# A four-way column and row scan: the order of batches, rows and columns of the map in SBUF

## The chip, the cores and the metric

The kernel runs on one core of a Trainium2 chip. A core has five engines that run at the same time and wait for each other by semaphores: TensorE (matrix products, PE in the profile, with its weight loads as PEld), VectorE (DVE), ScalarE (ACT), GpSimd (POOL) and SyncE (SP, which here issues the DMAs). Tiles lie in SBUF, whose 128 partitions each hold a row of bytes; products land in PSUM. The metric is the device time of one execution in microseconds; less is better. All data is fp32.

## The reference

The input x has the shape [32 batches, 48 channels, 64 rows, 128 columns]. Two layers follow each other, each x = x + scan(groupnorm(x)). The scan of a layer goes over the map four times: down the rows, up the rows, right over the columns, left over the columns. Each step adds to a row (or column) a 5-tap convolution, over the other axis and all channels, of the row (or column) before it:

```python
def step(w, b):
    def f(carry, inp):
        nxt = inp + _conv1d(carry, w, b)   # 48 -> 48 channels, 5 taps, padding 2
        return (nxt, nxt)
    return f
...
xs = jnp.moveaxis(x, 2, 0)
d0 = xs[0]
_, d_rest = jax.lax.scan(step(down_w, down_b), d0, xs[1:])
D = jnp.concatenate([d0[None], d_rest], 0)
seq = jnp.concatenate([D[Hh - 3::-1], D[Hh - 1:Hh]], 0)
u0 = D[Hh - 1]
_, u_rest = jax.lax.scan(step(down_w, down_b), u0, seq)
...
ws = jnp.moveaxis(jnp.moveaxis(U, 0, 2), 3, 0)
_, r_rest = jax.lax.scan(step(right_w, right_b), r0, ws[1:])
...
_, l_rest = jax.lax.scan(step(left_w, left_b), l0, R[Ww - 2::-1])
...
x = x + _L0_conv_ref(_gn(x), ...)
x = x + _L1_conv_ref(_gn(x), ...)
```

The steps of a scan depend on each other, and so do the four scans and the two layers. The 32 batches are independent.

## The kernel before

**Layout.** Positions along the convolved axis go in pairs. The channels of the even position lie on partitions 0 to 47, those of the odd position on 64 to 111, zeros between (`SIDES`). One convolution step is then three accumulated 112 x 112 products (L173, L174, L177): with the pair itself, the pair before and the pair after. Each product appears twice in the trace, as two passes of TensorE over the same columns.

**Chains and lanes.** Four batches (G = 4) make a chain, whose steps are done together: a step in the down and up scans has 4 x 64 = 256 columns (64 pairs of columns of the map), one in the right and left scans 4 x 32 = 128 (32 pairs of rows). Eight chains go in two lanes: lane 0 has chains 0, 2, 4, 6 and lane 1 has 1, 3, 5, 7. The lanes are written step by step in turn, so that lane 1's products run while lane 0's step is finished on VectorE, and the other way round. Tile names carry chain, layer and scan: `ps_7L0d` is chain 7, layer 0, down.

**The map.** Each lane has one map (L75) that holds a chain's four batches, and the scans run in place on it. Its free dimensions are [batch G, pair of columns WP = 64, parity r, pair of rows HP = 32], 64 KB a partition. `row(h)`, L194, is a step's operand in down and up: 256 values, each 256 bytes from the next within a batch. `col(v)`, L197, is that of right and left: four runs of 32 values. `last` (L79) and the carries of the up scan are packed tiles of their own, [G, WP].

**A step** (`step`, L168) is the three products into a PSUM tile and one VectorE operation (L180) that adds bias and input and writes the result. In down it reads and writes the map; the last step writes `last`. In up the products read the packed carry, VectorE reads a row of the map and writes the next carry, and ScalarE copies each carry to where the other layout has it (`place`, L184, two copies a step, L188). In right and left VectorE reads and writes columns of the map.

**Between the scans.** Per batch: the input x is loaded to a tile [112, 32 pairs of rows, 128 columns] (L98, SyncE's queue), `add_scan` (L105) adds the map to it on GpSimd, `store_x` writes it out (L103), `stats` (L110) forms scale and offset of the group norm on VectorE, TensorE and ScalarE, and `normalize` (L148) writes the normalized batch into the map: four instructions, two on ScalarE (L152) for the even columns and two on GpSimd (L159) for the odd ones. From layer 0 to 1 the normalized batch is the one that was just added; from layer 1 the next chain's batch is loaded instead. The order of each engine's queue is laid down when the program is built, and each engine takes its instructions in that order.

Of the kernel before, what the change touches and what calls it, by code (L numbers as in the profile page):

```python
"""Two pre-activation layers x + scan(groupnorm(x)), each scan running down, up, right and
left over the feature map with a 5-tap convolution across the other axis per step.

Layout. Channels of even and odd positions along the convolved axis sit side by side on the
partitions (even at 0..47, odd at 64..111, zeros between), so that one convolution step is
three accumulated 112 x 112 matrix products: with the pair before, the pair itself and the
pair after. The map of a batch lies in SBUF as [pair of w][r][pair of h]:
  down/up:     partition side = parity of w, r = parity of h
  right/left:  partition side = parity of h, r = parity of w
The scans run in place; the up scan writes its rows to where the second layout has them.  # L10

Batches go in chains of G, and two chains are in flight step by step in turn, so that what
a step of one chain waits for runs under the other's matrix products.
"""
# [1 line left out]

# [5 lines left out]
F32 = mybir.dt.float32  # L22
AF = mybir.ActivationFunctionType
ALU = mybir.AluOpType
# [3 lines left out]
P = ODD + C  # L28
# [3 lines left out]
G = 4  # L32
# [7 lines left out]
def kernel(  # L40
# [31 lines left out]
        for i in range(LANES)  # L72
    ]
    maps = [
        cpool.tile([P, G, WP, 2, HP], F32, tag=f"map{i}", name=f"map{i}")  # L75
        for i in range(LANES)
    ]
    lasts = [
        cpool.tile([P, G, WP], F32, tag=f"last{i}", name=f"last{i}") for i in range(LANES)  # L79
    ]  # L80
    mid = dram.tile([B, C, H, W], F32, tag="mid", name="mid")

    # The partitions between the two sides carry zeros throughout.
    for i, t in enumerate(maps + [xt for lane in xts for xt in lane]):
        eng = nc.vector if i % 2 else nc.gpsimd
        eng.memset(t[32:64], 0.0)
# [5 lines left out]
        return ap[b].rearrange("c (q r) w -> r c q w", r=2)[side]  # L92

    def load_x(lane: int, src: bass.AP, b: int) -> bass.AP:
        """Batch j of a chain always goes to tile j % NX of its lane."""
        xt = xts[lane][b % G % NX]
        for side in range(2):
            nc.sync.dma_start(xt[SIDES[side]], rows(src, b, side))  # L98
        return xt
# [3 lines left out]
            nc.sync.dma_start(rows(dst, b, side), xt[SIDES[side]])  # L103

    def add_scan(lane: int, j: int, xt: bass.AP):  # L105
        nc.gpsimd.tensor_tensor(  # L106
            xt, xt, maps[lane][:, j].rearrange("c p r q -> c q (p r)"), ALU.add
        )

    def stats(xt: bass.AP, key: str):  # L110
        """Per-partition scale and offset of the group norm of one batch."""

        def small(n, name):
            return stat_pool.tile([P, n], F32, tag=name, name=f"{name}_{key}")

        st = stat_pool.tile([P, NSEG, 6], F32, tag="st", name=f"st_{key}")
        flat = xt.rearrange("c q w -> c (q w)")
        for s in range(NSEG):
            nc.vector.bn_stats(st[:, s, :], flat[:, bass.ts(s, SEG)])  # L119
        mv = small(2, "mv")  # L120
        nc.vector.bn_aggr(mv, st.rearrange("c s k -> c (s k)"))  # L121
        ps = ps_stat.tile([P, 2], F32, tag="ps_stat", name=f"ps_stat_{key}")
        nc.tensor.matmul(ps[:, 0:1], mask_sb, mv[:, 0:1], start=True, stop=True)  # L123
        mean = small(1, "mean")
        nc.vector.tensor_copy(mean, ps[:, 0:1])
        dev = small(1, "dev")
        nc.vector.tensor_sub(dev, mv[:, 0:1], mean)
        sq = small(1, "sq")
        nc.vector.scalar_tensor_tensor(sq, dev, dev, mv[:, 1:2], ALU.mult, ALU.add)  # L129
        nc.tensor.matmul(ps[:, 1:2], mask_sb, sq, start=True, stop=True)  # L130
        var = small(1, "var")
        nc.vector.tensor_scalar(var, ps[:, 1:2], GN_EPS, None, ALU.add)  # L132
        # 1 / sqrt(var), with a Newton step behind the table's square root.
        std = small(1, "std")
        nc.scalar.activation(std, var, AF.Sqrt)  # L135
        r0 = small(1, "r0")
        nc.vector.reciprocal(r0, std)
        t0 = small(1, "t0")
        nc.vector.scalar_tensor_tensor(t0, var, r0, r0, ALU.mult, ALU.mult)
        t1 = small(1, "t1")  # L140
        nc.vector.tensor_scalar(t1, t0, -0.5, 1.5, ALU.mult, ALU.add)
        scale = small(1, "scale")
        nc.vector.tensor_mul(scale, r0, t1)
        offset = small(1, "offset")
        nc.vector.scalar_tensor_tensor(offset, mean, -1.0, scale, ALU.mult, ALU.mult)  # L145
        return scale, offset

    def normalize(lane: int, j: int, xt: bass.AP, scale: bass.AP, offset: bass.AP):  # L148
        view = xt.rearrange("c q (p r) -> c p r q", r=2)
        for hs in range(2):  # L150
            hsl = SIDES[hs]
            nc.scalar.activation(  # L152
                maps[lane][SIDES[0], j, :, hs, :],
                view[hsl, :, 0, :],
                AF.Identity,
                bias=offset[hsl],
                scale=scale[hsl],
            )
            nc.gpsimd.tensor_scalar(  # L159
                maps[lane][SIDES[1], j, :, hs, :],  # L160
                view[hsl, :, 1, :],
                scale[hsl],
                offset[hsl],
                ALU.mult,
                ALU.add,
            )

    def step(lane: int, layer: int, way: int, key: str, prev, inp, dst):  # L168
        """dst = inp + conv(prev) + bias over [P, G, pairs]."""
        n = prev.shape[2]  # L170
        ps = ps_scan.tile([P, G, n], F32, tag=f"ps{lane}", name=f"ps_{key}")
        wt = w_sb[:, layer, way]
        nc.tensor.matmul(ps, wt[:, 1], prev, start=True, stop=False)  # L173
        nc.tensor.matmul(  # L174
            ps[:, :, 1:n], wt[:, 0], prev[:, :, 0 : n - 1], start=False, stop=False
        )
        nc.tensor.matmul(  # L177
            ps[:, :, 0 : n - 1], wt[:, 2], prev[:, :, 1:n], start=False, stop=True
        )
        nc.vector.scalar_tensor_tensor(  # L180
            dst, ps, b_sb[:, layer, way : way + 1], inp, ALU.add, ALU.add
        )

    def place(lane: int, h: int, carry: bass.AP):  # L184
        """Row h of the up scan to where the right and left scans read it."""
        q, hs = divmod(h, 2)
        for ws in range(2):
            nc.scalar.copy(maps[lane][SIDES[hs], :, :, ws, q], carry[SIDES[ws]])  # L188

    def scan(lane: int, layer: int, key: str, early):  # L190
        """The four scans of a layer. early() is called shortly before the end."""
        m, last = maps[lane], lasts[lane]

        def row(h):  # L194
            return m[:, :, :, h % 2, h // 2]

        def col(v):  # L197
            return m[:, :, v // 2, v % 2, :]

        for h in range(1, H):  # L200
            dst = row(h) if h < H - 1 else last
            step(lane, layer, DOWN, f"{key}d{h}", row(h - 1), row(h), dst)
            yield
        place(lane, H - 1, last)
        prev = last
        for h in range(H - 2, -1, -1):
            carry = carry_pool.tile(
                [P, G, WP], F32, tag=f"carry{lane}", name=f"carry_{key}u{h}"
            )
            inp = row(h - 1) if h else last  # L210
            step(lane, layer, DOWN, f"{key}u{h}", prev, inp, carry)
            place(lane, h, carry)
            prev = carry
            yield
        for v in range(1, W):
            step(lane, layer, RIGHT, f"{key}r{v}", col(v - 1), col(v), col(v))
            yield
        for v in range(W - 2, -1, -1):
            if v == 24:
                early()  # L220
            step(lane, layer, LEFT, f"{key}l{v}", col(v + 1), col(v), col(v))
            yield
# [43 lines left out]


def _weights(np, inputs):
    """[in side and channel, layer, way, pair offset, out side and channel]: the taps by
    the distance of the positions; zeros where the kernel does not reach."""  # L270
    w = np.zeros((P, 2, 3, 3, P), np.float32)
    b = np.zeros((P, 2, 3), np.float32)
    for layer in range(2):
# [11 lines left out]


def _group_mask(np):
    """Averages the partitions of a channel group, over both sides."""
    group = np.full(P, -1)
    for s in SIDES:  # L290
        group[s] = np.arange(C) // (C // GROUPS)
    same = (group[:, None] == group[None, :]) & (group[:, None] >= 0)
    return np.where(same, np.float32(GROUPS / (2 * C)), np.float32(0))
# [21 lines left out]
```

## Time and profile before

| | us |
|---|---|
| three runs, median (lowest, highest) | 8434.96 (8434.68, 8440.88) |
| profiled execution, span from the first to the last instruction | 8440.7 |
| chain 7, layer 0: down, first to first product load of the next scan | 315.4 |
| the same for up | 169.4 |
| the same for right | 172.6 |
| left, to its last product load | 168.8 |
| from there to chain 7's first product load in layer 1 | 200.1 |

The profiled execution's span is 5.7 us above the median of the runs and 0.2 below the highest of them; no other time is shown for it. TensorE is busy 6745.4 us (80% of the span), its weight loads 5026.5 (60%), VectorE 3721.4 (44%), ScalarE 1902.0 (23%), GpSimd 1264.6 (15%). The stages of the table come eight times, once for each pair of chains and each layer, with the two lanes interleaved. Shares over the whole span mix these stages; a row of the table of windows gives the busy times within one stage.

A group's row in the trace reads: line, engine, operation, output<-inputs, shapes, count | busy us, mean ns of one | idle time of the engine ahead of them and what ended it. A timeline row reads: start, length, engine, line, operation, and in brackets the idle time ahead with what ended it.

### The profile page before, as it was taken

To read this page: it belongs to the slowest core of one execution; us is meant where nothing else is said; L and a number is where in the kernel's file an instruction comes from. 1 tells how busy PE (TensorE), PEld (TensorE's weight loads), DVE (VectorE), ACT (ScalarE), POOL (GpSimd) and SP (SyncE) were. 2 spreads that over 40 slices of the span, in tenths; PEclk is the share of its full clock that TensorE was granted. 3 is DMA by queue.
4 is the path that set the end of the run, shared out by engine and by line. 5 is a ranking of instruction groups with operands and counts; after the bars stand their busy time and mean duration, and the time that the engine had idled before them with its cause. 6 is when DMAs were issued, how large, how long until landed. Compare 5 with 4: busy or idle time off the path is not lost. (4 is left out here: it accounts for less than half of the span.)

```text
span 8440.7 us, 85243 instructions
## 1 busy us (share of the span) xinstructions
PE 6745.4 (80%) x36736; PEld 5026.5 (60%) x36736; DVE 3721.4 (44%) x7235; ACT 1902.0 (23%) x2241; POOL 1264.6 (15%) x199
## 2 busy tenths in 40 slices
PE   4999559994499955999449995599944999559993
PEld 2479524894247952489424795248942479524893
DVE  5345533553334553355333455335532345533552
ACT  3070110700207011070020701107012070110700
POOL 4000330003300033000330003300043000330004
PEclk9999779997699977999769997799976999779997
DMA  9000240005700024000570002400057000340005
GB/s 94 0 1 1 44 76 0 1 1 74 105 0 1 1 41 79 0 1 1 75 105 0 1 1 46 74 0 1 1 75 105 0 1 1 46 74 0 1 1 90
DMA packets 497403, 258.09 MB, mean 31 GB/s; under 512 B 5392, under 2 KB 496912, under 8 KB 497024
## 3 DMA queue, kind: packets, MB, share of 16 engines
q1 hardware_dynamic: 496640, 251.68, 20.7%
q8 instruction: 287, 4.70, 0.2%
q10 hardware_dynamic: 384, 0.96, 0.0%
q14 instruction: 92, 0.75, 0.0%
HBM read 151.95 MB, written 100.66 MB: 30 GB/s over the span
## 5 line engine op out<-in xcount | busy, mean ns | idle before, releaser
L106 POOL TENSOR_TENSOR x<-x,map 112x4096 f32<-112x4096 f32 x64 | 694.3, 10866 | 6611.4 <-issue 3290.5
L123 PE MATMUL ps_stat_x<-mv_x,mask_sb 112*112 112x1 f32 x64 | 16.4, 326 | 728.1 <-DVE mv_x L121 722.2
L188 ACT COPY map<-last 48x256 f32<-48x256 f32 x32 | 21.9, 683 | 2469.5 <-DVE last L180 2469.2
L123 PEld LDWEIGHTS ps_stat_x<-mv_x,mask_sb 112*112 112x112 f32 x64 | 14.9, 286 | 731.8 <-DVE mv_x L121 724.8
L135 ACT ACTIVATE std_m<-var_m 112x1 f32<-112x1 f32 x32 | 6.5, 203 | 1850.4 <-DVE var_m L132 1850.3
L123 PE MATMUL ps_stat_m<-mv_m,mask_sb 112*112 112x1 f32 x64 | 16.4, 326 | 473.8 <-DVE mv_m L121 448.6
L119 DVE BATCH_NORM_STATS2 st_x<-x 112x6 f32<-112x512 f32 x256 | 155.6, 679 | 513.9 <-DMA x<-in_x 513.7
L135 ACT ACTIVATE std_x<-var_x 112x1 f32<-112x1 f32 x32 | 6.5, 203 | 1615.1 <-DVE var_x L132 1615.1
L159 POOL TENSOR_SCALAR map<-x,scale_x,offset_x 48x2048 f32<-48x2048 f32 x64 | 277.8, 4341 | 346.3 <-DVE offset_x L145 340.3
L119 DVE BATCH_NORM_STATS2 st_m<-x 112x6 f32<-112x512 f32 x256 | 160.5, 679 | 340.7 <-POOL x L106 340.7
L159 POOL TENSOR_SCALAR map<-x,scale_m,offset_m 48x2048 f32<-48x2048 f32 x64 | 271.6, 4244 | 195.4 <-DVE offset_m L145 171.3
L123 PEld LDWEIGHTS ps_stat_m<-mv_m,mask_sb 112*112 112x112 f32 x64 | 14.9, 286 | 477.7 <-DVE mv_m L121 450.7
L152 ACT ACTIVATE map<-x,offset_x,scale_x 48x2048 f32<-48x2048 f32 x64 | 279.3, 4364 | 44.9 <-DVE offset_x L145 41.3
L152 ACT ACTIVATE map<-x,offset_m,scale_m 48x2048 f32<-48x2048 f32 x64 | 273.1, 4268 | 51.6 <-DVE offset_m L145 34.1
L130 PE MATMUL ps_stat_m<-sq_m,mask_sb 112*112 112x1 f32 x64 | 16.5, 328 | 151.9 <-DVE sq_m L129 151.9
L180 DVE SCALAR_TENSOR_TENSOR map<-ps_1L1d,b_sb,map 112x256 f32<-112x256 f32 x62 | 75.3, 1215 | 123.7 <-PE ps_1L1d L177 117.9
L180 DVE SCALAR_TENSOR_TENSOR map<-ps_3L1d,b_sb,map 112x256 f32<-112x256 f32 x62 | 75.5, 1217 | 123.1 <-PE ps_3L1d L177 118.0
L180 DVE SCALAR_TENSOR_TENSOR map<-ps_7L0d,b_sb,map 112x256 f32<-112x256 f32 x62 | 76.3, 1231 | 121.2 <-PE ps_7L0d L177 115.6
L180 DVE SCALAR_TENSOR_TENSOR map<-ps_7L1d,b_sb,map 112x256 f32<-112x256 f32 x62 | 75.5, 1217 | 123.0 <-PE ps_7L1d L177 117.9
L180 DVE SCALAR_TENSOR_TENSOR map<-ps_5L1d,b_sb,map 112x256 f32<-112x256 f32 x62 | 75.4, 1216 | 123.0 <-PE ps_5L1d L177 117.9
L180 DVE SCALAR_TENSOR_TENSOR map<-ps_3L0d,b_sb,map 112x256 f32<-112x256 f32 x62 | 76.4, 1232 | 120.7 <-PE ps_3L0d L177 115.4
L180 DVE SCALAR_TENSOR_TENSOR map<-ps_5L0d,b_sb,map 112x256 f32<-112x256 f32 x62 | 76.3, 1231 | 120.6 <-PE ps_5L0d L177 115.5
(617 smaller groups left out, 19622.9 us busy)
## 6 DMA issues: line engine op xcount, KB each, us to landing
x<-in_x SPq DMA_DIRECT2D x128, 768.0 KB, 16.3
mid<-x SPq DMA_DIRECT2D x64, 768.0 KB, 12.1
x<-mid SPq DMA_DIRECT2D x64, 768.0 KB, 16.0
out<-x SPq DMA_DIRECT2D x64, 768.0 KB, 12.6
w_sb<-in_w ACTq DMA_DIRECT2D x1, 882.0 KB, 12.2
mask_sb<-in_mask ACTq DMA_DIRECT2D x1, 49.0 KB, 1.9
b_sb<-in_b ACTq DMA_DIRECT2D x1, 2.6 KB, 5.4
```

The lines of the kernel that those rows point to most:

```text
L106: nc.gpsimd.tensor_tensor(xt, xt, maps[lane][:, j].rearrange("c p r q -> c q (p r)"), ALU.add)
L119: nc.vector.bn_stats(st[:, s, :], flat[:, bass.ts(s, SEG)])
L123: nc.tensor.matmul(ps[:, 0:1], mask_sb, mv[:, 0:1], start=True, stop=True)
L130: nc.tensor.matmul(ps[:, 1:2], mask_sb, sq, start=True, stop=True)
L135: nc.scalar.activation(std, var, AF.Sqrt)
L152: nc.scalar.activation(maps[lane][SIDES[0], j, :, hs, :], view[hsl, :, 0, :], AF.Identity, bias=offset[hsl], scale=scale[hsl],)
L159: nc.gpsimd.tensor_scalar(maps[lane][SIDES[1], j, :, hs, :], view[hsl, :, 1, :], scale[hsl], offset[hsl], ALU.mult, ALU.add,)
L180: nc.vector.scalar_tensor_tensor(dst, ps, b_sb[:, layer, way : way + 1], inp, ALU.add, ALU.add)
L188: nc.scalar.copy(maps[lane][SIDES[hs], :, :, ws, q], carry[SIDES[ws]])
```

## The change

The map's free dimensions become [parity r, pair of columns, pair of rows, batch], so that the four batches of a chain lie side by side. `row(h)` is then 64 runs of four values (16 bytes), each run 512 bytes from the next; `col(v)` is one run of 128 values. `last`, the carries and the PSUM tiles follow: [pairs, batch]. The products with the pair before and after are shifted by one pair of four columns, so that their PSUM output is one run. `normalize` reads x along the columns in steps of 8 bytes and writes the map in steps of 512. `add_scan` becomes two instructions for each batch, one for each parity r, that read and write x in steps of 8 bytes and read the map in steps of 512. `place` writes rows of runs of 16 bytes. Sizes of tiles, loads, stores and the arithmetic stay. Comments are left out of the new file.

```diff
     maps = [
-        cpool.tile([P, G, WP, 2, HP], F32, tag=f"map{i}", name=f"map{i}")
+        cpool.tile([P, 2, WP, HP, G], F32, tag=f"map{i}", name=f"map{i}")
...
-        cpool.tile([P, G, WP], F32, tag=f"last{i}", name=f"last{i}") for i in range(LANES)
+        cpool.tile([P, WP, G], F32, tag=f"last{i}", name=f"last{i}") for i in range(LANES)
...
     def add_scan(lane: int, j: int, xt: bass.AP):
-        nc.gpsimd.tensor_tensor(
-            xt, xt, maps[lane][:, j].rearrange("c p r q -> c q (p r)"), ALU.add
-        )
+        for r in range(2):
+            half = xt.rearrange("c q (p r) -> c r q p", r=2)[:, r]
+            nc.gpsimd.tensor_tensor(half, half, maps[lane][:, r, :, :, j].rearrange("c p q -> c q p"), ALU.add)
...
     def normalize(lane: int, j: int, xt: bass.AP, scale: bass.AP, offset: bass.AP):
-        view = xt.rearrange("c q (p r) -> c p r q", r=2)
+        view = xt.rearrange("c q (p r) -> c r q p", r=2)
...
             nc.scalar.activation(
-                maps[lane][SIDES[0], j, :, hs, :],
-                view[hsl, :, 0, :],
+                maps[lane][SIDES[0], hs, :, :, j].rearrange("c p q -> c q p"),
+                view[hsl, 0],
...
             nc.gpsimd.tensor_scalar(
-                maps[lane][SIDES[1], j, :, hs, :],
-                view[hsl, :, 1, :],
+                maps[lane][SIDES[1], hs, :, :, j].rearrange("c p q -> c q p"),
+                view[hsl, 1],
...
-        ps = ps_scan.tile([P, G, n], F32, tag=f"ps{lane}", name=f"ps_{key}")
+        ps = ps_scan.tile([P, n, G], F32, tag=f"ps{lane}", name=f"ps_{key}")
...
         nc.tensor.matmul(
-            ps[:, :, 1:n], wt[:, 0], prev[:, :, 0 : n - 1], start=False, stop=False
+            ps[:, 1:n], wt[:, 0], prev[:, 0 : n - 1], start=False, stop=False
         )
...
         for ws in range(2):
-            nc.scalar.copy(maps[lane][SIDES[hs], :, :, ws, q], carry[SIDES[ws]])
+            nc.scalar.copy(maps[lane][SIDES[hs], ws, :, q], carry[SIDES[ws]])
...
         def row(h):
-            return m[:, :, :, h % 2, h // 2]
+            return m[:, h % 2, :, h // 2]
...
         def col(v):
-            return m[:, :, v // 2, v % 2, :]
+            return m[:, v % 2, v // 2]
```

More of the change, by code (lines that the diff above doesn't have):

```diff
@@ L168, in step @@
     def step(lane: int, layer: int, way: int, key: str, prev, inp, dst):
-        n = prev.shape[2]
-        ps = ps_scan.tile([P, G, n], F32, tag=f"ps{lane}", name=f"ps_{key}")
+        n = prev.shape[1]
+        ps = ps_scan.tile([P, n, G], F32, tag=f"ps{lane}", name=f"ps_{key}")
         wt = w_sb[:, layer, way]
@@ L174, in step @@
         nc.tensor.matmul(
-            ps[:, :, 1:n], wt[:, 0], prev[:, :, 0 : n - 1], start=False, stop=False
+            ps[:, 1:n], wt[:, 0], prev[:, 0 : n - 1], start=False, stop=False
         )
         nc.tensor.matmul(
-            ps[:, :, 0 : n - 1], wt[:, 2], prev[:, :, 1:n], start=False, stop=True
+            ps[:, 0 : n - 1], wt[:, 2], prev[:, 1:n], start=False, stop=True
         )
@@ L207, in scan @@
             carry = carry_pool.tile(
-                [P, G, WP], F32, tag=f"carry{lane}", name=f"carry_{key}u{h}"
+                [P, WP, G], F32, tag=f"carry{lane}", name=f"carry_{key}u{h}"
             )
```

## The prediction

> **What bounds the kernel now.** The trace is first cut into stages: a table of windows inside the seventh and eighth chain's first layer (down, up, right, left), then two between scans. Columns: window and length, busy time of the engines with instruction counts, granted clock, DMA share, GB/s.
>
> ```profile
> core 0: us, PE busy (x) PEld busy (x) DVE busy (x) ACT busy (x) POOL busy (x), PEclk, DMA share, GB/s
> 6480.00:6770.00 290.00, 289.70 (x678) 130.72 (x677) 113.97 (x114) 0.00 (x0) 0.00 (x0) 1.00 0.00 0
> 6785.00:6940.00 155.00, 155.00 (x710) 120.32 (x708) 81.78 (x118) 150.84 (x232) 0.00 (x0) 1.00 0.00 1
> 6950.00:7115.00 165.00, 165.00 (x1467) 165.00 (x1467) 85.59 (x244) 0.00 (x0) 0.00 (x0) 0.99 0.01 1
> 7292.00:7455.00 163.00, 7.47 (x28) 6.29 (x28) 79.35 (x126) 52.43 (x19) 124.69 (x19) 0.51 0.64 105
> 4100.00:4330.00 230.00, 7.47 (x28) 6.28 (x28) 50.54 (x126) 55.68 (x20) 139.91 (x21) 0.51 0.96 141
> ```
>
> In all scans TensorE is busy without a gap at full clock, so a scan costs what its matrix passes cost; between scans TensorE is idle and GpSimd and the DMAs set the pace. Down and up do the same arithmetic (same weights, same 256 and 252 columns), yet down needs 290 us for 678 recorded passes and up 155 us for 710. Then the length of one step, from VectorE's starts of one lane in the timeline of down, and the extent of down and up on lane 1 (per-tile view: min/median/max ns, first and last start):
>
> ```profile
> 6759.73 0.76 DVE L180 SCALAR_TENSOR_TENSOR map<-ps_6L0d,b_sb,map 112x256 f32<-112x256 f32 x1 [1.30 <-PE ps_6L0d L177]
> 6762.29 1.26 DVE L180 SCALAR_TENSOR_TENSOR map<-ps_7L0d,b_sb,map 112x256 f32<-112x256 f32 x1 [1.80 <-PE ps_7L0d L177]
> 6764.85 0.76 DVE L180 SCALAR_TENSOR_TENSOR map<-ps_6L0d,b_sb,map 112x256 f32<-112x256 f32 x1 [1.30 <-PE ps_6L0d L177]
> ...
> L173 PEld LDWEIGHTS ps_7L0d<-map,w_sb x126: 173/193/307, 6463.1 to 6774.9; 112*112 112x112 f32 x126
> L173 PEld LDWEIGHTS ps_7L0u<-last,w_sb x2: 177/177/177, 6778.5 to 6778.8; 112*112 112x112 f32 x2
> L173 PEld LDWEIGHTS ps_7L0u<-carry_7L0u,w_sb x124: 172/177/177, 6781.1 to 6941.6; 112*112 112x112 f32 x124
> L173 PEld LDWEIGHTS ps_7L1d<-map,w_sb x126: 172/193/307, 7489.4 to 7798.6; 112*112 112x112 f32 x126
> L173 PEld LDWEIGHTS ps_7L1u<-last,w_sb x2: 177/177/177, 7802.3 to 7802.5; 112*112 112x112 f32 x2
> ```
>
> A step of both lanes in down takes 6764.85 - 6759.73 = 5.12 us, that is twelve passes (three products, two passes each, two lanes) of 427 ns, 1.67 ns a column of 256. In up it is (6941.6 - 6781.1) / 62 = 2.59 us, 216 ns a pass, 0.84 ns a column. What differs is the moving operand: up reads a packed carry, down reads a row of the map in which each value lies 256 bytes from the next. In right, 165 us for 1467 passes is 112 ns for 124 or 128 columns, 0.9 ns: runs of 32 values are already at the packed rate.
>
> **The change, part by part.**
>
> *Down's products.* The row becomes 64 runs of 16 bytes at steps of 512. No row of before shows such runs. Bounds: 216 ns a pass (packed) and 427 ns (every value apart). I take the packed end: one location apart costs 1.67 ns, and four columns at 0.84 take 3.34 ns, twice as long, in which the fetch of the next run can hide. Lane 1's down, first load to the first load of up, takes 6778.5 - 6463.1 = 315.4 us in layer 0 and 7802.3 - 7489.4 = 312.9 in layer 1, mean 314.2, or 61.4 steps of both lanes. Each saves 5.12 - 2.59 = 2.53 us: 155 us, and over the eight pairs of chain and layer **-1243 us**.
>
> [...]
>
> *VectorE in down.* What must hide it is the other lane's six passes, 1.28 us after the change.
>
> ```profile
> L180 DVE SCALAR_TENSOR_TENSOR map<-ps_7L0d,b_sb,map 112x256 f32<-112x256 f32 x58 | 72.5, 1250 | 108.3 <-PE ps_7L0d L177 108.3
> L180 DVE SCALAR_TENSOR_TENSOR map<-ps_6L0d,b_sb,map 112x256 f32<-112x256 f32 x56 | 43.1, 769 | 70.0 <-PE ps_6L0d L177 69.9
> L180 DVE SCALAR_TENSOR_TENSOR carry_7L0u<-ps_7L0u,b_sb,map 112x256 f32<-112x256 f32 x59 | 40.9, 694 | 36.7 <-ACT map L188 21.8 <-PE ps_7L0u L177 14.9
> L188 ACT COPY map<-carry_7L0u 48x256 f32<-48x256 f32 x116 | 75.6, 652 | 2.1
> ...
> L180 DVE SCALAR_TENSOR_TENSOR carry_7L0u<-ps_7L0u,b_sb,last x1: 483/483/483, 6943.4 to 6943.4; 112x256 f32<-112x256 f32 x1
> L180 DVE SCALAR_TENSOR_TENSOR last<-ps_7L0d,b_sb,map x1: 657/657/657, 6777.7 to 6777.7; 112x256 f32<-112x256 f32 x1
> L180 DVE SCALAR_TENSOR_TENSOR map<-ps_7L0r,b_sb,map x127: 350/351/353, 6949.6 to 7120.1; 112x128 f32<-112x128 f32 x127
> ```
>
> With all operands packed the operation took 483 ns, with one apart 657, with two 769 on lane 0 and 1250 on lane 1. Lane 1 works on row h while TensorE reads row h of the other map, lane 0 on a row of the other parity; I read the difference as a collision of the two in the memory, with TensorE served first, since its pass is 427 ns under either. After the change the operation lies between 483 and 1250 ns. I take about 650, the row with one operand apart: hidden, 0. At 1250 ns with some 0.13 us of hand-over (an estimate from VectorE's 0.05 to 0.1 us on either side in the timelines) the lane's own chain would be 1.28 + 1.25 + 0.13 = 2.66 us against 2.59: +0.07 x 61.4 x 8 = +34 us, my upper end.
>
> *Up.* Products read the packed carry as before. ScalarE's copies (L188), 652 ns with outputs 256 bytes apart, were busy 150.84 of 155 us, and VectorE waits for them half the time; they now write runs. The bounds are no gain and the whole difference between 2.59 and twelve passes of 213 ns, 2.56 us: 0.03 x 62 x 8 = 15. I take **-8 us**. Were the copies to get slower instead (two per lane and step), each 10 ns would add 0.04 us to the step, 20 us in all; nothing here makes them so.
>
> *Right and left.* Columns become one run of 128 values. The passes (112 ns) are at the packed rate, VectorE's 351 ns lies on the line through 483 (133 ns less for 128 values less, 1.04 ns each). 0, within 5 ns a step either way: 5 ns x 254 x 8 = 10 us.
>
> *Between the scans* the same bytes are touched in another order. GpSimd's queue carries it:
>
> ```profile
> L106 POOL TENSOR_TENSOR x<-x,map x64: 10842/10851/11107, 962.5 to 8407.4; 112x4096 f32<-112x4096 f32 x64
> L159 POOL TENSOR_SCALAR map<-x,scale_m,offset_m x64: 3790/4214/4852, 1009.7 to 7489.4; 48x2048 f32<-48x2048 f32 x64
> L152 ACT ACTIVATE map<-x,offset_m,scale_m x64: 3823/4238/4895, 1009.7 to 7489.3; 48x2048 f32<-48x2048 f32 x64
> ...
> 14.43 6.96 POOL L86 MEMSET x<- 32x4096 f32 x2
> ...
> 7290.10 43.27 POOL L106 TENSOR_TENSOR x<-x,map 112x4096 f32<-112x4096 f32 x4 [822.77 <-issue]
> 7337.37 8.81 POOL L159 TENSOR_SCALAR map<-x,scale_m,offset_m 48x2048 f32<-48x2048 f32 x2 [4.00 <-DVE offset_m L145]
> 7351.37 9.35 POOL L159 TENSOR_SCALAR map<-x,scale_m,offset_m 48x2048 f32<-48x2048 f32 x2 [5.18 <-DVE dev_m L127]
> ...
> 7314.05 8.53 DVE L127 TENSOR_TENSOR dev_m<-mv_m,mean_m 112x1 f32<-112x1 f32 x1
> 7323.11 10.28 DVE L129 SCALAR_TENSOR_TENSOR sq_m<-dev_m,mv_m 112x1 f32<-112x1 f32 x1
> ```
>
> Normalize read 512 bytes apart and wrote runs of 128 bytes; now it reads 8 bytes apart and writes 512 apart. ScalarE's copy shows that spaced writes cost about what spaced reads do: 652 / 256 = 2.5 ns a value with its start, normalize's spaced read 4238 / 2048 = 2.1. One spaced stream goes and one comes: 0. The add read x packed and the map 128 bytes apart; now x in steps of 8 bytes and the map 512 apart, still one spaced stream, in two instructions instead of one. A second start: between 0 and 0.3 us; at 0.15 x 64, **+10 us**.
>
> Splitting the add has an answer on VectorE. Two of its 1-element operations took 8.53 and 10.28 us beside the adds; they ended at 7322.58 and 7333.39, when the third and fourth add end (7290.10 + n x 43.27 / 4), so each waited for the add in progress, and the first two normalizes then started 4.00 and 5.18 us late. With halves such a wait is for a half. I take 5 us for each of the four boundaries from layer 0 to 1, **-20 us**, bounds 0 and 9 each. The others wait for loads (DMA share 0.96): 0. The DMAs, their order and their bytes stay; the loads of x and the stores behind the adds move only with the adds.
>
> **Sum**, against the profiled execution's span: 8440.7 - 1243 - 8 + 10 - 20 = 7180. The median of the runs, 8434.96, is 5.7 below that span; keeping the difference, **7174**. Its own range, by the bounds above, is 7110 to 7240.
>
> **The rivals.**
>
> *A run has a price of its own.* If the first column of each run costs 1.67 ns and only the other three 0.84, a pass is 64 x 4.19 = 268 ns and a step 3.22 us: 1.90 x 61.4 x 8 = 933 saved instead of 1243, **7484**. For it: no row has runs this short with the same low address bits. Against it: 3.34 ns to hide 1.67.
>
> *The boundary gets dearer.* If reads in 8-byte steps are no cheaper than spaced ones, normalize has two spaced streams and the add one more. VectorE's second spaced stream cost 769 - 657 = 112 ns, its first 174 ns for 256 values, 0.4 to 0.7 ns each; TensorE's 0.84. At 0.8: +1.6 us for each of 128 normalize instructions, +3.3 for each of 64 adds, **+416**, 7590.
>
> *The boundary gets cheaper.* If only spaced reads cost, normalize on GpSimd falls towards a packed write (6.96 / 2 = 3.48 us for 4096 values in the memset, 1.74 for 2048). Half way from 4.2, 3.0 us: 1.2 x 128 = 154 less, **7020**. [...] ScalarE's spaced writes speak against it.
>
> *Slower: the step decides, not the run.* All 64 runs lie 512 bytes apart, and lane 1's 1250 ns shows that equal low address bits collide. If each column then pays 1.67 ns still, a pass stays at 427 ns, nothing is saved, and the boundary with its 512-byte steps pays the 416 of above: **8850**. It is slower as soon as a pass stays above 427 - 416 / (61.4 x 12 x 8) = 356 ns. Against it: the steps of 256 and 512 bytes in L188 and L152 cost nearly alike today.
>
> *It does not reach the bound*: down's rate comes from something other than the operand, so 8435. Up, with equal products, speaks against it.
>
> **How the numbers follow.** Forecast 0.60, run price 0.17, dearer boundary 0.11, cheaper boundary 0.07, slower 0.03, no change 0.02. The range takes in the forecast, the cheaper boundary and the run price, 7010 to 7490, and leaves out 0.16. Some 0.2% is what a measurement of this kernel can tell from no change; faster 0.95, same 0.02, slower 0.03.
>
> **What would show it.** Right: in down the step of both lanes at 2.6 us, VectorE's L180 there under 0.8 us and alike on both lanes, L188 well under 652 ns, L159 and L152 near 4.2 us, L106 as 128 instructions near 5.4 us, the time between scans about as now. Wrong: passes in down well above 216 ns, or L106 and L159 lengthened by more than a tenth, which moves every boundary.

## The result and the profile after

The changed kernel takes 7177.3 us (median of 4 runs, 7174.2 to 7184.59) against 8437.92 of the kernel before on the same chip: a ratio of 0.8506, 95% interval 0.8494 to 0.8518. The prediction was 7174. The profiled execution has a span of 7178.1 us, 1262.6 less than before.

First the table of windows of the kernel after, in the columns of the prediction: the same four stages of the seventh and eighth chain (down, up, right, the stretch from layer 0 to 1).

```profile
5530.00:5665.00 135.00, 135.00 (x634) 111.86 (x633) 51.09 (x106) 0.00 (x0) 0.00 (x0) 1.00 0.00 1
5680.00:5825.00 145.00, 145.00 (x681) 120.14 (x680) 54.72 (x114) 91.57 (x227) 0.00 (x0) 1.00 0.00 1
5840.00:6000.00 160.00, 160.00 (x1435) 160.00 (x1434) 83.84 (x239) 0.00 (x0) 0.00 (x0) 1.00 0.00 1
6175.00:6350.00 175.00, 7.47 (x28) 6.29 (x28) 77.69 (x126) 48.35 (x20) 140.36 (x27) 0.51 0.62 98
```

TensorE is still busy throughout the scans, but a pass in down now costs 135 / 634 = 213 ns (before: 290 us for 678 records, 427 ns by the length of a step), the same as in up. In up ScalarE has room: 91.57 of 145 us, where it had 150.84 of 155. Its copies there, by the groups in a window of up after, take 404 ns instead of 652:

```profile
L188 ACT COPY map<-carry_7L0u 48x256 f32<-48x256 f32 x102 | 41.3, 404 | 24.1 <-DVE carry_7L0u L180 23.5
```

In the last row of the table GpSimd is busier than before, 80% of the window against 76%.

The per-tile view of chain 7 after (min/median/max ns, first and last start) gives the length of each stage on lane 1:

```profile
L173 PEld LDWEIGHTS ps_7L0d<-map,w_sb x126: 172/177/307, 5511.4 to 5669.6; 112*112 112x112 f32 x126
L173 PEld LDWEIGHTS ps_7L0u<-last,w_sb x2: 177/177/177, 5672.0 to 5672.2; 112*112 112x112 f32 x2
L173 PEld LDWEIGHTS ps_7L0u<-carry_7L0u,w_sb x124: 177/177/177, 5674.6 to 5831.1; 112*112 112x112 f32 x124
L173 PEld LDWEIGHTS ps_7L0r<-map,w_sb x254: 172/174/177, 5833.6 to 6002.6; 112*112 112x112 f32 x127
L177 PEld LDWEIGHTS ps_7L0l<-map,w_sb x254: 177/177/177, 6004.3 to 6173.2; 112*112 112x112 f32 x127
L173 PEld LDWEIGHTS ps_7L1d<-map,w_sb x126: 172/177/312, 6385.3 to 6542.7; 112*112 112x112 f32 x126
L180 DVE SCALAR_TENSOR_TENSOR map<-ps_7L0d,b_sb,map x62: 483/484/486, 5515.3 to 5668.6; 112x256 f32<-112x256 f32 x62
```

Two rows of the same view of the kernel before, where right begins and left ends:

```profile
L173 PEld LDWEIGHTS ps_7L0r<-map,w_sb x254: 172/176/310, 6947.9 to 7119.2; 112*112 112x112 f32 x127
L177 PEld LDWEIGHTS ps_7L0l<-map,w_sb x254: 177/177/177, 7120.9 to 7289.8; 112*112 112x112 f32 x127
```

Down takes 5672.0 - 5511.4 = 160.6 us instead of 315.4. The products of a step now also write one run in PSUM, but that is not what sped them up: in the kernel before, up wrote the same PSUM tile in four runs and took 216 ns a pass. Formed so from lane 1's rows of all eight pairs of chain and layer, and summed:

| stage, sum of eight (us) | before | after | difference |
|---|---|---|---|
| down | 2513.2 | 1281.8 | -1231.4 |
| up, with the way into right | 1355.3 | 1293.1 | -62.2 |
| right | 1378.5 | 1362.0 | -16.5 |
| left, to its last weight load | 1354.6 | 1354.8 | +0.2 |
| four stretches from layer 0 to 1 | 800.8 | 849.8 | +49.0 |
| three stretches from layer 1 to the next chain | 773.6 | 775.8 | +2.2 |
| start and end | 264.7 | 260.8 | -3.9 |

They add up to the 1262.6 us. The gain is down's, and two smaller entries cancel in part: the scans won 79 us beside down, and the stretches from layer 0 to 1 lost 49.

The loss is on GpSimd. Its rows and ScalarE's of normalize in the source views after, and the head of the timeline of GpSimd and VectorE in the stretch from layer 0 to 1:

```profile
L108 POOL TENSOR_TENSOR x<-x,map x128: 6939/6944/6966, 789.9 to 7155.1; 112x2048 f32<-112x2048 f32 x128
L159 POOL TENSOR_SCALAR map<-x,scale_m,offset_m x64: 3763/3848/3977, 847.0 to 6385.2; 48x2048 f32<-48x2048 f32 x64
L152 ACT ACTIVATE map<-x,offset_m,scale_m x64: 3807/3900/3970, 847.0 to 6385.2; 48x2048 f32<-48x2048 f32 x64
...
6172.20 55.27 POOL L108 TENSOR_TENSOR x<-x,map 112x2048 f32<-112x2048 f32 x8 [657.00 <-issue]
6227.99 7.76 POOL L159 TENSOR_SCALAR map<-x,scale_m,offset_m 48x2048 f32<-48x2048 f32 x2 [0.52 <-DVE offset_m L145]
6240.77 7.78 POOL L159 TENSOR_SCALAR map<-x,scale_m,offset_m 48x2048 f32<-48x2048 f32 x2 [5.01 <-DVE dev_m L127]
...
6202.17 4.61 DVE L127 TENSOR_TENSOR dev_m<-mv_m,mean_m 112x1 f32<-112x1 f32 x1
6207.31 6.38 DVE L129 SCALAR_TENSOR_TENSOR sq_m<-dev_m,mv_m 112x1 f32<-112x1 f32 x1
6215.64 4.95 DVE L139 SCALAR_TENSOR_TENSOR t_m<-var_m,r_m 112x1 f32<-112x1 f32 x1
6221.77 5.72 DVE L143 TENSOR_TENSOR scale_m<-r_m,t_m 112x1 f32<-112x1 f32 x1
```

An add is two instructions of 6.94 us, 13.9 together, against 10.85. Normalize became shorter, median 3.85 us against 4.21. In the first batch of this stretch four of VectorE's small operations now last to the end of half an add (4.61, 6.38, 4.95 and 5.72 us; the first ends at 6202.17 + 4.61 = 6206.78, the fifth half at 6172.20 + 5 x 55.27 / 8 = 6206.74), where two lasted to the end of an add before (8.53 and 10.28 us).

### The profile page after: what moved, and what is told of

Its sections match the earlier page's. It is cut to its first block, busy times and chain, and to the rows that moved or that the text cites. A ratio compares the mean times of both kernels' runs of the same rounds, so it can differ in the third digit from the quotient of the medians.

```text
span 7178.1 us, 85349 instructions
## 1 busy us (share of the span) xinstructions
PE 5461.0 (76%) x36736; PEld 4945.8 (69%) x36736; DVE 2983.2 (42%) x7235; ACT 1339.9 (19%) x2241; POOL 1397.9 (19%) x263
## 4 chain that ended last, share of the span: by engine, by line
PE 74%; POOL 8%; DVE 6%; SPq 4%; DMA 3%; issue 2%; ACT 1%; POOLq 0%; DVEq 0%; ACTq 0%
POOL x L108 6%; DMA x<-in_x 3%; POOL map L159 2%; SPq L103 2%; DVE st_m L119 2%; SPq L98 2%; ACT map L152 1%; DVE st_x L119 1%; DVE sq_m L129 1%; PE ps_1L0r L173 0%; PE ps_5L1r L173 0%; PE ps_1L1r L173 0%; PE ps_7L0r L173 0%; PE ps_7L1r L173 0%; PE ps_3L1r L173 0%
## 5 line engine op out<-in xcount | busy, mean ns | idle before, releaser
L108 POOL TENSOR_TENSOR x<-x,map 112x2048 f32<-112x2048 f32 x128 | 884.7, 6946 | 5275.5 <-issue 2627.9
L123 PE MATMUL ps_stat_x<-mv_x,mask_sb 112*112 112x1 f32 x64 | 16.5, 327 | 746.3 <-DVE mv_x L121 740.2
L123 PE MATMUL ps_stat_m<-mv_m,mask_sb 112*112 112x1 f32 x64 | 16.5, 327 | 560.4 <-DVE mv_m L121 492.5
L159 POOL TENSOR_SCALAR map<-x,scale_x,offset_x 48x2048 f32<-48x2048 f32 x64 | 246.4, 3850 | 308.5 <-DVE offset_x L145 302.6
L159 POOL TENSOR_SCALAR map<-x,scale_m,offset_m 48x2048 f32<-48x2048 f32 x64 | 245.9, 3842 | 179.6 <-DVE offset_m L145 156.2
L152 ACT ACTIVATE map<-x,offset_m,scale_m 48x2048 f32<-48x2048 f32 x64 | 248.4, 3881 | 93.2 <-DVE offset_m L145 75.8
L152 ACT ACTIVATE map<-x,offset_x,scale_x 48x2048 f32<-48x2048 f32 x64 | 248.9, 3889 | 43.9 <-DVE offset_x L145 40.3
L130 PEld LDWEIGHTS ps_stat_m<-sq_m,mask_sb 112*112 112x112 f32 x64 | 14.4, 286 | 112.3 <-DVE sq_m L129 112.3
L180 DVE SCALAR_TENSOR_TENSOR map<-ps_7L0r,b_sb,map 112x128 f32<-112x128 f32 x127 | 44.6, 351 | 44.8 <-PE ps_7L0r L177 44.8
L180 DVE SCALAR_TENSOR_TENSOR map<-ps_1L0r,b_sb,map 112x128 f32<-112x128 f32 x127 | 44.6, 351 | 44.8 <-PE ps_1L0r L177 44.8
L180 DVE SCALAR_TENSOR_TENSOR map<-ps_5L1r,b_sb,map 112x128 f32<-112x128 f32 x127 | 44.6, 351 | 44.8 <-PE ps_5L1r L177 44.8
L180 DVE SCALAR_TENSOR_TENSOR map<-ps_3L1r,b_sb,map 112x128 f32<-112x128 f32 x127 | 44.6, 351 | 44.8 <-PE ps_3L1r L177 44.8
L180 DVE SCALAR_TENSOR_TENSOR map<-ps_1L1r,b_sb,map 112x128 f32<-112x128 f32 x127 | 44.6, 351 | 44.8 <-PE ps_1L1r L177 44.8
L180 DVE SCALAR_TENSOR_TENSOR map<-ps_7L1r,b_sb,map 112x128 f32<-112x128 f32 x127 | 44.6, 351 | 44.8 <-PE ps_7L1r L177 44.8
```

What stands on the lines that cost most here:

```text
L108: nc.gpsimd.tensor_tensor(half, half, maps[lane][:, r, :, :, j].rearrange("c p q -> c q p"), ALU.add)
L152: nc.scalar.activation(maps[lane][SIDES[0], hs, :, :, j].rearrange("c p q -> c q p"), view[hsl, 0], AF.Identity, bias=offset[hsl], scale=s ...
L159: nc.gpsimd.tensor_scalar(maps[lane][SIDES[1], hs, :, :, j].rearrange("c p q -> c q p"), view[hsl, 1], scale[hsl], offset[hsl], ALU.mult, ...
L180: nc.vector.scalar_tensor_tensor(dst, ps, b_sb[:, layer, way : way + 1], inp, ALU.add, ALU.add)
```

## Experiments

Each is a variant of the kernel before or after. "Stretch" is lane 1's time from the last weight load of left in layer 0 to the first of down in layer 1, chain 7: 7489.4 - 7289.8 = 199.6 us before and 6385.3 - 6173.2 = 212.1 after.

### The add in one instruction, x packed (changed kernel)

```diff
-        for r in range(2):
-            half = xt.rearrange("c q (p r) -> c r q p", r=2)[:, r]
-            nc.gpsimd.tensor_tensor(half, half, maps[lane][:, r, :, :, j].rearrange("c p q -> c q p"), ALU.add)
+        full = xt.rearrange("c q (p r) -> c q p r", r=2)
+        nc.gpsimd.tensor_tensor(
+            full, full, maps[lane][:, :, :, :, j].rearrange("c r p q -> c q p r"), ALU.add
+        )
```

> The changed kernel with the add of a batch as one GpSimd instruction over x packed (4096 values), the map read in the new layout. Theory (the 8-byte steps in x made the add dearer, 6.94 us for each half): one instruction near 10.9 us, as before the change, and the time from lane 1's last product load of left to its first of down, layer 0 to 1, falls from 212.5 us to 195 to 200 (adds 3 us shorter, normalize stays 3.85); over four such boundaries some 50 to 70 us, a time of 7110 to 7130. Rival (the map's steps of 512 bytes instead of 128 made it dearer): 13.9 us, and a time within 10 us of 7177.

7074.87 us (4 runs), ratio to the kernel before 0.8378 (0.8364 to 0.8392), about 102 us better than the change. The source view of this kernel:

```profile
L107 POOL TENSOR_TENSOR x<-x,map x64: 10844/10849/10908, 793.5 to 7049.4; 112x4096 f32<-112x4096 f32 x64
```

10.85 us with the map in its new place, where the walk goes 32 KB from one parity to the other and 512 bytes from pair to pair: that cost what steps of 128 did, and the rival falls. (Steps of 512 alone, with x packed, were not run.) The stretch is 6293.4 - 6100.6 = 192.8 us. The time lies 35 to 55 us below the expected one, which counted four stretches at 12.5 to 17.5 us each. A stretch has the adds of both lanes in its queue, eight and not four; all four stretches together fell by 79 us (849.8 to 770.9), and the three from layer 1 on, which were not counted, by 18 (775.8 to 757.9).

### The add in two halves by parity (kernel before)

```diff
-        nc.gpsimd.tensor_tensor(
-            xt, xt, maps[lane][:, j].rearrange("c p r q -> c q (p r)"), ALU.add
-        )
+        for r in range(2):
+            half = xt.rearrange("c q (p r) -> c r q p", r=2)[:, r]
+            nc.gpsimd.tensor_tensor(
+                half, half, maps[lane][:, j, :, r].rearrange("c p q -> c q p"), ALU.add
+            )
```

> The kernel before with the add alone split in two halves by the parity of the column, x in 8-byte steps, the map as before (steps of 256 bytes). Theory (8-byte steps in x): two instructions of 6.9 us, the boundary from layer 0 to 1 grows from 200 to 212 us or more, a time of 8480 to 8500. Rival (steps of the map): two of 5.4 us, the boundary shrinks by the 5 us that the prediction gave the split, 8415 to 8435.

8546.18 us, ratio 1.0123 (1.0108 to 1.0138): 103 us slower, 46 to 66 more than expected, by the same slip: the four stretches grew by 87 us in sum (800.8 to 888.0). In its source view:

```profile
L108 POOL TENSOR_TENSOR x<-x,map x128: 6990/7002/7022, 961.7 to 8519.8; 112x2048 f32<-112x2048 f32 x128
```

The stretch is 222.1 us. The two parts of the change there come apart, to within some 3 us:

| stretch (us) | add whole | add split by parity |
|---|---|---|
| map and normalize as before | 199.6 | 222.1 |
| map and normalize as changed | 192.8 | 212.1 |

### Two halves with x packed (changed kernel)

That leaves two causes in the split: the 8-byte steps, or the second instruction. Here the halves are the first and the last 16 pairs of rows.

```diff
-        for r in range(2):
-            half = xt.rearrange("c q (p r) -> c r q p", r=2)[:, r]
-            nc.gpsimd.tensor_tensor(half, half, maps[lane][:, r, :, :, j].rearrange("c p q -> c q p"), ALU.add)
+        full = xt.rearrange("c q (p r) -> c q p r", r=2)
+        scan = maps[lane][:, :, :, :, j].rearrange("c r p q -> c q p r")
+        for k in range(2):
+            part = slice(k * HP // 2, (k + 1) * HP // 2)
+            nc.gpsimd.tensor_tensor(full[:, part], full[:, part], scan[:, part], ALU.add)
```

> The changed kernel with the add again in two instructions of 2048 values, but split by pairs of rows instead of the column's parity, so that x stays packed and the map is read as in the run of the whole add. Theory (the 8-byte steps in x cost 1.5 us a half, the second instruction nothing): two of 5.4 us, lane 1's stretch from layer 0 to 1 near the 192.7 us of the whole add or a few less, 7065 to 7085. Rival (the cost is that of a second instruction): two of 6.9 us, 212 us, 7177.

7040.35 us in one run. In its source view:

```profile
L110 POOL TENSOR_TENSOR x<-x,map x128: 5508/5517/5556, 794.7 to 7012.0; 112x2048 f32<-112x2048 f32 x128
```

5.52 us a half, 11.0 for both: the second instruction costs 0.2 us, and the steps 6.94 - 5.52 = 1.43 us a half, 0.70 ns a value. The stretch falls to 6248.8 - 6068.2 = 180.6, 12 us under the whole add, where "a few" were expected. The statistics run over segments of four pairs of rows, so four of the eight need only the first half and can begin while GpSimd adds the second; that they do is read from the waits, no row here shows VectorE in that run. Normalize waits 6.4 us behind each of three late adds and 7.6 behind the fourth, where it waits 8.8 and 9.9 behind whole adds, and 0.22 us instead of 4.00 at its first start. Together that is some 13 us, less 1 for the second instructions. The first start and one late wait in the timeline of GpSimd, in brackets, this kernel first, then that of the whole add:

```profile
6112.52 7.74 POOL L161 TENSOR_SCALAR map<-x,scale_m,offset_m 48x2048 f32<-48x2048 f32 x2 [0.22 <-DVE offset_m L147]
6167.95 7.72 POOL L161 TENSOR_SCALAR map<-x,scale_m,offset_m 48x2048 f32<-48x2048 f32 x2 [6.43 <-DVE offset_m L147]
```

```profile
6148.15 7.74 POOL L160 TENSOR_SCALAR map<-x,scale_m,offset_m 48x2048 f32<-48x2048 f32 x2 [4.00 <-DVE offset_m L146]
6205.80 7.74 POOL L160 TENSOR_SCALAR map<-x,scale_m,offset_m 48x2048 f32<-48x2048 f32 x2 [8.80 <-DVE offset_m L146]
```

Whether reading or writing x in 8-byte steps costs the time was not tried.

### Normalize alone in the changed order (kernel before)

```diff
-        view = xt.rearrange("c q (p r) -> c p r q", r=2)
+        view = xt.rearrange("c q (p r) -> c r q p", r=2)
...
-                maps[lane][SIDES[0], j, :, hs, :],
-                view[hsl, :, 0, :],
+                maps[lane][SIDES[0], j, :, hs, :].rearrange("c p q -> c q p"),
+                view[hsl, 0],
```

(The same for GpSimd's instruction.)

> The kernel before with normalize alone walking as in the changed kernel, along the columns in the inner loop: x read in 8-byte steps instead of 512, the map written in steps of 256 bytes instead of runs. In the changed kernel a normalize instruction takes 3.84 us on GpSimd against 4.2 to 4.4 before. Theory (ScalarE and GpSimd read the same partitions of x side by side, and reads 512 bytes apart get in each other's way, while their writes go to different partitions): 3.84 us here too, the stretch from layer 0 to 1 falls from 200 to about 193 us, and the time by 20 to 50 us. Rival (it is the place of the map's bytes, not the order of the walk): 4.2 to 4.4 and 200 us as before.

8387.3 us in one run, against 8437.35 of the kernel before. In its source view:

```profile
L159 POOL TENSOR_SCALAR map<-x,scale_m,offset_m x64: 3750/3876/3922, 1007.0 to 7434.8; 48x2048 f32<-48x2048 f32 x64
```

The stretch is 7434.9 - 7241.2 = 193.7 us. The order of the walk is what shortens normalize, by 50 us in all, and the place of the map is not needed for it. The shortest instruction hardly moves (3.79 us before, 3.75 here), the longest does (4.85 to 3.92). That would fit engines getting in each other's way. VectorE is not needed for it: in the kernel before, two instructions of GpSimd's ran while VectorE did nothing (0.00 in the table of windows), and one of them took 4.21 us, the other 3.83.

```profile
7427.28:7435.40 8.12, 0.00 (x0) 0.00 (x0) 0.00 (x0) 8.00 (x2) 8.04 (x2) 0.50 0.22 35
L159 POOL TENSOR_SCALAR map<-x,scale_m,offset_m x2: 3834/4022/4210, 7427.3 to 7431.6; 48x2048 f32<-48x2048 f32 x2
```

What ran beside both is ScalarE's part of normalize and some DMAs (share 0.22); which of them lengthens the instruction was not tried.

### Half of the up scan's copies on GpSimd (kernel before)

```diff
-            nc.scalar.copy(maps[lane][SIDES[hs], :, :, ws, q], carry[SIDES[ws]])
+            dst = maps[lane][SIDES[hs], :, :, ws, q]
+            if ws:
+                nc.gpsimd.tensor_copy(dst, carry[SIDES[ws]])
+            else:
+                nc.scalar.copy(dst, carry[SIDES[ws]])
```

> The kernel before with one of the two copies of the up scan's carry on GpSimd instead of ScalarE. Theory (ScalarE's copies held up back, at 652 ns each they filled 151 of 155 us): a step of both lanes in up falls from 2.59 to 2.52 us, up from its first product load to right's first falls from 169.4 to about 162 us, and eight of them give 60 us: 8375. Rival (up got faster because VectorE's operation there fell from 694 to 484 ns, which stays at 694 here): up stays at 169 us, 8435.

8368.55 us, ratio 0.9913 (0.9898 to 0.9928): 75 us less. Up, formed as in the table of stages, takes 161.9 us in chain 7, layer 0, right 170.3, as in the changed kernel. The groups in a window of up (chain 7, layer 0):

```profile
L192 ACT COPY map<-carry_7L0u 48x256 f32<-48x256 f32 x41 | 25.8, 630 | 26.7 <-DVE carry_7L0u L180 26.7
L190 POOL COPY map<-carry_7L0u 48x256 f32<-48x256 f32 x41 | 25.5, 621 | 27.1 <-DVE carry_7L0u L180 27.1
L180 DVE SCALAR_TENSOR_TENSOR carry_7L0u<-ps_7L0u,b_sb,map 112x256 f32<-112x256 f32 x39 | 25.4, 651 | 24.6 <-PE ps_7L0u L177 24.6
```

VectorE's operation takes 651 ns, not the 484 of the changed kernel, and waits for TensorE alone now; so the rival falls, by which up got faster through VectorE's shorter operation. ScalarE's queue was a second bound of up in the kernel before, beside TensorE, and its late copies also held up the first product of right (on lane 0 it waited 3.53 us for a copy in the kernel before): 2.8 us lie between up's last first-product load and right's here (6883.0 - 6880.2), where it was 6.3.

### Lane 1's map 128 bytes further on (kernel before)

```diff
-        cpool.tile([P, G, WP, 2, HP], F32, tag=f"map{i}", name=f"map{i}")
+        cpool.tile([P, 32 * i + G * WP * 2 * HP], F32, tag=f"map{i}", name=f"map{i}")[
+            :, 32 * i :
+        ].rearrange("c (g p r q) -> c g p r q", g=G, p=WP, r=2)
```

> The kernel before with lane 1's map 128 bytes further on in SBUF, nothing else. Theory of the prediction (lane 1's operation in down takes 1250 ns and lane 0's 769 because lane 1 works on a row with the same low address bits as the row that TensorE reads): the two swap, lane 0 near 1250 ns and lane 1 near 769. Rival (it hangs on the order of the lanes, not on addresses): as before, 769 and 1250. The time stays within 10 us of 8437 under either, since both are hidden.

VectorE's groups in a window of down (chains 6 and 7, layer 0):

```profile
L182 DVE SCALAR_TENSOR_TENSOR map<-ps_6L0d,b_sb,map 112x256 f32<-112x256 f32 x50 | 60.0, 1199 | 86.8 <-PE ps_6L0d L179 86.7
L182 DVE SCALAR_TENSOR_TENSOR map<-ps_7L0d,b_sb,map 112x256 f32<-112x256 f32 x51 | 39.1, 766 | 74.8 <-PE ps_7L0d L179 74.8
```

The long operation moved from lane 1 (1250 ns) to lane 0 (1199): here it went with the addresses, although lane 0's own map did not move. Of the other engines only TensorE is at work in down (ScalarE and GpSimd 0.00 in the table of windows before). The time, 8459.31 us in one run, lies 13 us over the highest run of the kernel before, outside the 10 us that were expected; down is 316.5 us in layer 0 and 314.5 in layer 1 of chain 7, against 315.4 and 312.9, which times eight is most of it. Why down got longer is not shown.

### Runs of 8 bytes (changed kernel)

```diff
-        cpool.tile([P, 2, WP, HP, G], F32, tag=f"map{i}", name=f"map{i}")
+        cpool.tile([P, 2, 2, WP, HP, 2], F32, tag=f"map{i}", name=f"map{i}")
...
-            return m[:, h % 2, :, h // 2]
+            return m[:, h % 2, :, :, h // 2]
```

(The carries, `last` and the PSUM tile are [pair of batches, pairs, batch of the pair].)

> The changed kernel with only two batches side by side: the map is [parity r, pair of batches, pair of columns, pair of rows, batch of the pair], so that a row in down is 128 runs of 8 bytes at steps of 256. It asks how short a run may be. By two columns at the packed 0.84 ns, 1.67 ns a run, which is what one location apart costs, the step stays at 2.52 us (down 160 us). By a price for each run (1.67 ns for its first column, 0.84 for the other) a pass takes 128 x 2.51 = 321 ns and the step 3.85 us, down 237 us, 610 us more in all. VectorE's operation in down between 484 ns and 769. The rest as in the changed kernel, but for the last dimension of right's and left's columns, now two runs of 64 values.

7187.65 us in one run; down is 161.7 and 160.9 us in chain 7. The groups in a window of down:

```profile
L180 DVE SCALAR_TENSOR_TENSOR map<-ps_7L0d,b_sb,map 112x256 f32<-112x256 f32 x47 | 33.5, 713 | 29.8 <-PE ps_7L0d L177 29.8
L180 DVE SCALAR_TENSOR_TENSOR map<-ps_6L0d,b_sb,map 112x256 f32<-112x256 f32 x47 | 30.7, 653 | 27.0 <-PE ps_6L0d L177 27.0
L173 PE MATMUL ps_6L0d<-map,w_sb 112*112 112x256 f32 x94 | 27.9, 377 | 0.0
```

A pass, with its overlap, reads 377 ns here. The same groups in windows of down of the kernel before, and of the kernel after:

```profile
L173 PE MATMUL ps_7L0d<-map,w_sb 112*112 112x256 f32 x115 | 60.0, 610 | 0.3 <-DVE map L180 0.3
```

```profile
L173 PE MATMUL ps_7L0d<-map,w_sb 112*112 112x256 f32 x106 | 31.5, 379 | 0.0
```

Runs of 16 and of 8 bytes read alike, 379 and 377 ns, and values apart 610. No price of a run shows on TensorE down to two values. VectorE does feel it, 653 and 713 ns instead of 484, hidden here.

### The whole add on VectorE, and shared (changed kernel)

The first is the one-instruction add with `nc.vector` for `nc.gpsimd`:

> The changed kernel with the whole add, x packed, on VectorE instead of GpSimd. VectorE's one packed and one spaced input would take 4096 x 1.7 = 7.0 us (its 657 ns for 256 values, with 0.2 us of start), against 10.85 on GpSimd. Theory (GpSimd's queue sets the stretch from layer 0 to 1, 148 of 193 us in the run of the whole add): adds and normalizes go side by side, the stretch falls to 150 to 180 us, a time of 6900 to 7040. Rival (VectorE's statistics and adds now queue behind each other, and an add with two inputs in SBUF waits for GpSimd's normalize as the small operations did): 190 us or more, 7060 to 7150.

6920.25 us (4 runs), ratio 0.8199 (0.8185 to 0.8212): the fastest version, about 257 us under the changed kernel. The stretch is 6131.3 - 5978.0 = 153.3 us. In the second, batches 0 and 2 of a chain are added on VectorE, and 1 and 3 on GpSimd in halves of packed x:

> The changed kernel with the adds of batches 0 and 2 of a chain on VectorE (one instruction, x packed) and those of 1 and 3 on GpSimd (two halves by pairs of rows). Theory (both engines' queues bound the stretch in turn, 181 us with all adds in halves on GpSimd, 153 with all on VectorE): sharing gives 140 to 153 us, a time of 6860 to 6920. Rival (the two engines' two-input operations and normalize wait for each other, so that GpSimd's adds only lengthen VectorE's): 155 to 180 us, 6930 to 7040.

6997.24 us, ratio 0.8289 (0.8276 to 0.8303): the rival. The stretch is 6189.6 - 6031.5 = 158.1 us, and the stretches from layer 1 on are longer too (264.5 against 249.2 ahead of chain 7). The adds in the groups of the first kernel, then the source views of the second:

```profile
L107 DVE TENSOR_TENSOR x<-x,map 112x4096 f32<-112x4096 f32 x64 | 459.4, 7190 | 141.2 <-DMA x<-mid 140.7
```

```profile
L109 DVE TENSOR_TENSOR x<-x,map x32: 7118/7228/12105, 791.9 to 6926.2; 112x4096 f32<-112x4096 f32 x32
L113 POOL TENSOR_TENSOR x<-x,map x64: 5505/5515/12435, 792.1 to 6966.5; 112x2048 f32<-112x2048 f32 x64
```

The medians are those of an add alone, 7.2 and 5.5 us; only the longest ones, 12.1 and 12.4, are far from them. The rows of x's tiles at the start of the stretch show why:

```profile
L109 DVE TENSOR_TENSOR x<-x,map x1: 7145/7145/7145, 6031.6 to 6031.6; 112x4096 f32<-112x4096 f32 x1
L113 POOL TENSOR_TENSOR x<-x,map x1: 12338/12338/12338, 6031.8 to 6031.8; 112x2048 f32<-112x2048 f32 x1
...
L109 DVE TENSOR_TENSOR x<-x,map x1: 11634/11634/11634, 6039.5 to 6039.5; 112x4096 f32<-112x4096 f32 x1
L113 POOL TENSOR_TENSOR x<-x,map x1: 12428/12428/12428, 6044.1 to 6044.1; 112x2048 f32<-112x2048 f32 x1
```

VectorE's first add ends at 6031.6 + 7.1 = 6038.8, and GpSimd's half, begun at 6031.8, ends 5.4 us after that, at 6044.2: it waited for the whole add and then took its usual time. VectorE's next add, begun at 6039.5, ends 7.0 us after that half, and GpSimd's second half 5.4 us after this add. In these rows the two engines took turns, each add at its usual length once the other was done, and an add that met one on the other engine gained nothing. GpSimd's normalize can be read in the same way in the first kernel: its longest instruction takes 10.96 us there, at a median of 3.87, and the 7.1 us between them are the length of an add (median 7.15).

## Why the prediction was right, and where it was not

The time came within 4 us, but three of the terms behind it were wrong by 50 to 92 us each: the copies in up and normalize gained more than forecast (71 and 50 us), and the add lost more (92). That it came so near is luck. (The bounds of its parts, added up, also give 7131 to 7255, not 7110 to 7240.)

- **Down's products, -1243 forecast, -1231 measured: right.** A pass goes to the packed rate, 213 ns. The rival of a price for each run is out at 16 bytes and, by the run with two batches side by side, at 8. That the fetch of the next run hides under the columns of the one before was the author's estimate; what the traces show is the length of a pass with its overlap: 379 ns with four fp32 values side by side, 377 with two, 610 with one.
- **VectorE in down, "I take about 650" ns: too long, and hidden as forecast.** It takes 484, the packed time, on both lanes. That the 1250 ns behind the upper bound hang on addresses was read rightly (with a shift of 128 bytes lane 0 takes 1199 ns and lane 1 766), but with runs of 16 bytes the difference is gone; that it is a collision in the memory, with TensorE served first, was the author's reading, which no run shows.
- **Up, "-8 us" with at most 15: mis-sized.** Up and the way into right gave 62, right another 16. Two slips made the bound too low. Twelve passes were put at 213 ns each, but eight of the twelve have 252 columns; the step after is (5831.1 - 5674.6) / 62 = 2.52 us, not 2.56. And right's first product waited for the last copies, which the sum left out: from up's last first-product load to right's was 6947.9 - 6941.6 = 6.3 us before and is 5833.6 - 5831.1 = 2.5 after. The mechanism, ScalarE's copies, was named and is right: moving half of them off ScalarE alone gave 75 us.
- **The add, "still one spaced stream, in two instructions", +10: wrong.** The second instruction costs 0.2 us, as forecast, but the steps of 8 bytes in x, which the sum put at nothing without a row that showed it, cost 1.43 us a half. With the split by parity that made 102 us (7177.3 against 7074.87; 103 on the kernel before). Of the dearer-boundary rival this half came true: +3.04 us an add, where it had said 3.3.
- **Normalize, "one spaced stream goes and one comes: 0": wrong.** It gained 50 us, by the order of the walk: 26 in the four stretches from layer 0 to 1 (774.6 against 800.8 in sum) and 21 in the three from layer 1 on (752.3 against 773.6), which the prediction had waiting for loads alone. Here the cheaper-boundary rival had the direction, but its reason does not show: the shortest instruction takes 3.79 us with reads 512 bytes apart and 3.75 with reads 8 bytes apart. A saving on the reads that the spaced writes ate up is not ruled out.
- **The split's answer on VectorE, -20: half seen.** The first normalize of the stretch waits 4.00 us with the add whole, 0.52 split by parity and 0.22 split by rows; the second waits 5.01 in all three. That is 3.5 us a stretch in the changed kernel, 14 in the four, and they are part of the 102 that the split by parity costs on balance. Split by rows, at no price in the add, it is worth 12 us a stretch; by the reading above, because the statistics can start after a half.

Down 1231, up and right 79, normalize 50, less 102 for the add: 1258 of the measured 1262.6, each from a comparison of its own. The forecast named the right stage and bound, and its nearness to within 4 us is owed to errors that cancel.

## What to carry to other kernels

Put side by side what one operand reads together: here two fp32 values next to each other already shortened the down scan from 315.4 to 161.7 us, and four, at 160.6 us, brought a pass of TensorE from 427 to 213 ns for 256 columns (1.67 to 0.83 ns a column), which was worth 15%. Then look at every other instruction that touches the same tile, engine by engine, with its own inner step: the new order left alone or helped TensorE's other scans, VectorE, ScalarE's copies and normalize, and the add lost 102 us, because its packed operand was given steps of 8 bytes without need. A bound that lies a few per cent under the main one (ScalarE in up, 97% busy) is worth pricing with the waits at the ends of the stage, not only by its share.

## What the runs showed of the hardware

- VectorE's operation on values 256 bytes apart took 769 ns on lane 0 and 1250 on lane 1, beside TensorE alone, which reads the other lane's map (on lane 1 the same row of an equally laid out map); with 128 bytes of shift it took 1199 and 766 ns. With runs of 16 bytes it took 484 ns on both.
- On GpSimd the two-input add in place took 2.65 ns a value with packed x (10.85 us / 4096) and 3.39 with x in steps of 8 bytes (6.94 / 2048); with packed x, steps of 128 bytes in the other input took what steps of 32 KB and 512 bytes in turn did (10.851 and 10.849 us), and with x in steps of 8 bytes, 256 and 512 differed by 0.03 ns a value (7002 against 6944 ns for 2048).
- Two-input adds on VectorE and GpSimd took turns by whole instructions: of GpSimd's 64 halves in the shared run 48 took 5.5 us and 16 took 12.3 to 12.4, and of VectorE's 32 adds 24 took 7.1 to 7.3 us and 8 took 11.6 to 12.1.
